# A gated-attention residual and LayerNorm kernel: the first group's own path through the statistics taken out, p added by VectorE or by accumulating transfers, and a new written order

## The chip, the cores and the metric

The kernel runs on one core of one Trainium2 chip. The metric is the device time of one execution in microseconds. One core has TensorE (PE; PEld are its weight loads), VectorE (DVE), ScalarE (ACT), GpSimd (POOL) and SyncE (SP), which here only issues transfers. Every engine works through its own instructions in the order in which they are written.

## The reference

The input x has 8 batches of 512 positions of 1024 values. Per batch, blocks of positions are summed, a key projection with Wk and a softmax over 8 blocks give weights, and the weighted block sum times Wo is one vector p per batch. All positions of the batch get it, then a LayerNorm and the residual follow:

```python
block_repr = inputs.reshape(B, n_blocks, block_size, H).sum(axis=2)
keys = jnp.einsum('bnh,kh->bnk', block_repr, Wk)
keys = keys / rms * rms_weight            # rms over the last axis
attn = jax.nn.softmax(jnp.einsum('bnh,h->bn', keys, q), axis=-1)
attended = jnp.einsum('bn,bnh->bh', attn, block_repr)
proj = jnp.einsum('bsh,kh->bsk', broadcast(attended), Wo)      # p
y = inputs + proj
out = (y - mu) / jnp.sqrt(var + EPS) * ln_gamma + ln_beta
return x + out
```

## The kernel before

The 8 batches form four groups of two. A group is 8 "rows" of work: a row is 128 partitions x 1024 values, and two rows make a tile of 1 MB. So there are 32 rows, 0 to 7 in the first group (group 0), 8 to 15 in group 1 and so on. They stay in the SBUF buffer xs, which has 26 places of one row (a weight tile takes one).

The loads come first: Wk, the four tiles of group 0, Wo, gamma, then the other groups as places come free. TensorE transposes the weights (L340, L351), sums blocks (L367, L389), projects (L411, L423) and spreads p over the partitions (L445, L499); the result is pb, one p per batch, in all partitions. Four rows of p go by four small GpSimd transfers into a table tab (L521).

Of a row of groups 1 to 3, `moments` adds p on VectorE and takes the row's sum in the same instruction (L556, called A here); ScalarE squares with that sum as bias (L559, the square). Several rows form a unit (UNITS: mostly four). For a unit GpSimd makes 1/std by a power, std by a product and writes columns into stat (`unit`, L627 to L635); TensorE transposes stat into lt. Then `results` ends a row: VectorE writes (gamma + std) * x into PSUM (L652, called B), TensorE adds the outer product of lt and tab (L642), ScalarE multiplies by 1/std into xs (L662), and SP stores two rows at once (L702). The last two rows go in halves (L674, L685).

Rows of group 0 go another way. Their own moments are taken by half-row statistics ahead of p, while the weights are still arriving (`x_moments`, L565, L567). p is not added to them; when p stands, one VectorE instruction per row takes the covariance with p (`x_cross`, L570, called C), p's moments come from L510 to L513, GpSimd joins them (`x_unit`, L582 to L597) and multiplies the table by a table of gamma (gtab, L525).

The order is not left to a scheduler. Each step is recorded with a number by `add`; the string ORDER lists the steps, each with a letter for its engine (G is GpSimd, S SP) and, behind an @, a place in xs or PSUM. A step is emitted, with all its instructions, where its token stands. Tokens like u4 are matrix products of zeros that nobody reads.

Of the kernel before, what the change touches and what calls it, by code (L numbers as in the profile page):

```python
# [9 lines left out]
AF = mybir.ActivationFunctionType  # L10
# [4 lines left out]
EPS = 1e-6  # L15
LAYER = 1
# [86 lines left out]
def block_attn_resid_kernel(  # L103
# [101 lines left out]
    cvt = alloc("cvt", [P, NX])
# [80 lines left out]
    for k in range(2):  # L286
        v = xpick[:, k, :].rearrange("p (r i m) -> p r i m", r=2, i=2)
        spots(v[:, :, :, 1 : 1 + GM], [[0, 2], [-2, 2], [0, GM]], -k, "xpick")
        for m in (0, GM + 1):
            spots(v[:, :, :, m : m + 1], [[0, 2], [0, 2], [0, 1]], -8, "xpick")  # L290
# [518 lines left out]
```

## Time and profile before

| | us |
|---|---|
| median of 3 runs (144.13 to 144.63) | 144.63 |
| the profiled execution | 144.32 |
| its span | 142.6 |
| PE busy (84%) | 119.7 |
| DVE busy (82%) | 116.6 |
| ACT busy (59%) | 83.9 |
| POOL busy (50%) | 71.3 |
| moved: 42.74 MB, mean over the span | 300 GB/s |

The profile shows one execution. Busy time is added over the whole span, so an engine at 82% may still be the limit of one stretch and idle in another. Between the profiled execution's own time and its span lie 1.7 us.

### The profile page before, as it was taken

What the parts mean: (1) busy time and instruction counts of PE and PEld (TensorE: products, weight loads), DVE (VectorE), ACT (ScalarE), POOL (GpSimd) and SP (SyncE); (2) the same over time, 40 slices, a digit from 0 to 9 for tenths busy, and PEclk for the clock granted to TensorE, in tenths of its full rate; (3) what the DMA queues carried; (4) which work ended last, traced back from release to release, by engine and by line L of the source; (5) the groups of instructions that cost most, each with busy time, mean ns of one, the idle gap of its engine ahead of it and who ended that gap; (6) DMA issues with size and microseconds to landing.
All of it is one profiled execution on the core that took longest, in us unless ns stands there. A gap on an engine that the chain in (4) does not pass through costs nothing.

```text
span 142.6 us, 2990 instructions
## 1 busy us (share of the span) xinstructions
PE 119.7 (84%) x1143; PEld 60.4 (42%) x1150; DVE 116.6 (82%) x194; ACT 83.9 (59%) x129; POOL 71.3 (50%) x106
## 2 busy tenths in 40 slices
PE   0999969999999996799999978998699774899920
PEld 0384439678865453334544242543243221323300
DVE  1269999999448997579999899999997999899900
ACT  3000050825833010173999979999978999699660
POOL 6881000000405788948223928993778069967100
PEclk9999999999999999879999999999959999999985
DMA  4999999999999998007785995617337708668894
GB/s 148 412 414 434 407 409 409 409 408 415 421 418 421 419 417 368 28 5 294 247 353 218 326 427 211 257 44 294 147 159 287 297 0 331 257 246 345 340 392 155
DMA packets 8286, 42.74 MB, mean 300 GB/s; under 512 B 1440, under 2 KB 1456, under 8 KB 4432
## 3 DMA queue, kind: packets, MB, share of 16 engines
q1 hardware_dynamic: 7632, 42.47, 73.8%
q8 instruction: 9, 0.15, 0.4%
q0 software_dynamic: 640, 0.08, 0.4%
q14 instruction: 5, 0.04, 0.1%
HBM read 25.71 MB, written 16.78 MB: 298 GB/s over the span
## 4 chain that ended last, share of the span: by engine, by line
DMA 29%; DVE 19%; PE 17%; POOL 16%; ACT 6%; issue 5%; SPq 2%; ACTq 0%; POOLq 0%; DVEq 0%
DMA xs<-in_L_cond_Wk_dram 11%; DMA xs<-in_x_dram 11%; DVE xs L556 11%; PE banks L642 7%; DMA xs<-in_L_cond_Wo_dram 7%; DVE banks L652 5%; PE banks L499 3%; ACT square L559 3%; PE banks L776 3%; POOL urs L631 3%; POOL stat L635 2%; POOL uv L629 2%; POOL ca L477 2%; PE banks L411 2%; DVE pb L570 2%
## 5 line engine op out<-in xcount | busy, mean ns | idle before, releaser
L652 DVE SCALAR_TENSOR_TENSOR banks<-gam,ustd,xs 128x1024 f32<-128x1024 f32 x30 | 38.7, 1320 | 1.9 <-ACT xs L662 0.9
L662 ACT ACTIVATE xs<-banks,urs 128x1024 f32<-128x1024 f32 x30 | 31.8, 1109 | 2.7 <-PE banks L642 2.3
L642 PE MATMUL banks<-tab,lt 32*128 32x512 f32 x128 | 27.8, 672 | 3.1 <-DVE banks L652 2.6
L556 DVE SCALAR_TENSOR_TENSOR xs<-xs,pb 128x1024 f32<-128x1024 f32 x24 | 28.8, 1220 | 0.9 <-ACT pb L167 0.8
L559 ACT ACTIVATE square<-xs,stat 128x1024 bf16<-128x1024 f32 x24 | 27.6, 1152 | 1.7 <-DVE xs L556 1.3
L776 PE MATMUL banks<-zeros 128*128 128x512 bf16 x69 | 20.3, 417 | 4.3 <-POOL blk L255 3.8
L477 POOL TENSOR_TENSOR ca<-cv,minus_half 128x8 f32<-128x8 f32 x4 | 9.5, 2382 | 27.8 <-DVE cv L475 27.7
L340 PE MATMUL banks<-ident,xs 128*128 128x128 f32 x120 | 15.7, 284 | 0.2 <-ACT wkT L167 0.2
L340 PEld LDWEIGHTS banks<-ident,xs 128*128 128x128 f32 x120 | 14.7, 195 | 2.7 <-issue 1.7
L411 PE MATMUL banks<-wkT,blkT 128*32 128x256 f32 x256 | 15.2, 381 | 0.4 <-DVE blkT L399 0.4
L167 ACT COPY wkT<-banks 128x1024 f32<-128x1024 f32 x3 | 2.9, 1015 | 21.0 <-PE banks L340 21.0
L642 PEld LDWEIGHTS banks<-tab,lt 32*128 32x128 f32 x128 | 8.3, 190 | 14.9 <-DVE banks L652 7.8
L521 POOL DMA_DIRECT2D tab<-pb x16 | 9.2, 577 | 9.6 <-ACT pb L167 9.6
L776 PEld LDWEIGHTS <-zeros 128*128 128x128 bf16 x74 | 6.9, 105 | 16.7 <-issue 8.9
L411 PE MATMUL banks<-woT,blkT 128*32 128x256 f32 x192 | 12.4, 397 | 0.0
L367 PE MATMUL banks<-xs,blk 128*32 128x256 f32 x192 | 12.2, 383 | 0.3 <-issue 0.3
L627 POOL COPY stat<-stat 128x4 f32<-128x4 f32 (+1 forms) x7 | 6.2, 879 | 10.2 <-DVE xs L556 5.1
L565 DVE BATCH_NORM_STATS2 bn<-xs 128x6 f32<-128x512 f32 x16 | 10.6, 686 | 0.2
L411 PEld LDWEIGHTS banks<-wkT,blkT 128*32 128x32 f32 x256 | 7.7, 110 | 6.3 <-DVE blkT L399 1.3
L570 DVE SCALAR_TENSOR_TENSOR pb<-xs,mv,pb 128x1024 f32<-128x1024 f32 x8 | 10.2, 1270 | 0.1
L629 POOL TENSOR_SCALAR uv<-ussq 128x4 f32<-128x4 f32 (+1 forms) x7 | 6.0, 864 | 5.6 <-ACT square L559 5.5
L631 POOL TENSOR_TENSOR urs<-uv,minus_half 128x4 f32<-128x4 f32 (+1 forms) x7 | 8.3, 1187 | 0.5
(103 smaller groups left out, 144.5 us busy)
## 6 DMA issues: line engine op xcount, KB each, us to landing
xs<-in_x_dram SPq DMA_DIRECT2D x16, 1024.0 KB, 13.1
out_dram<-xs SPq DMA_DIRECT2D x14, 1024.0 KB, 4.1
xs<-in_L_cond_Wk_dram SPq DMA_DIRECT2D x8, 512.0 KB, 13.1
xs<-in_L_cond_Wo_dram SPq DMA_DIRECT2D x8, 512.0 KB, 10.2
out_dram<-xs SPq DMA_DIRECT2D x2, 512.0 KB, 3.3
out_dram<-xs SPq DMA_DIRECT2D x4, 256.0 KB, 3.6
gam<-in_L_cond_ln_gamma_dram SPq DMA_DIRECT2D x1, 512.0 KB, 9.6
tab<-pb POOLq DMA_DIRECT2D x16, 4.0 KB, 3.5
```

The costliest lines, as they stand in the source:

```text
L340: nc.tensor.transpose(pair(name)[:, bass.ts(c, P)], xu(src)[:, c::HC], ident)
L367: nc.tensor.matmul(bank(name)[32 * j : 32 * j + 32, :QU], blk[G["g"]], xu(f"x{n}.{t}", r)[:, bass.ts(j, QU)], start=(t == 0 and r == 0), s ...
L411: nc.tensor.matmul(bank(name)[32 * j : 32 * j + 32, :QU], blkT[n % 2][:, c, :], wT[which][:, c, bass.ts(j, QU)], start=(c == 0), stop=(c = ...
L477: add("spow", "G", lambda _: nc.gpsimd.tensor_tensor(ca, cv, minus_half.to_broadcast([P, 8]), ALU.pow), reads=["cv", "minus_half"], writes ...
L556: add("A", "D", lambda _: nc.vector.scalar_tensor_tensor(x_row(k), x_row(k), 1.0, pb[n % 2], ALU.mult, ALU.add, accum_out=total), reads=pb ...
L559: add("Sq", "A", lambda _: nc.scalar.activation(square, x_row(k), AF.Square, bias=total, scale=-float(H), accum_out=ussq[u][:, r : r + 1]) ...
L570: add("C", "D", lambda _: nc.vector.scalar_tensor_tensor(pb[1], x_row(k), mv[:, k, 0:1], pb[0], ALU.subtract, ALU.mult, accum_out=cov[:, k ...
L631: add("upow", "G", lambda _: nc.gpsimd.tensor_tensor(rs, v, minus_half.to_broadcast([P, U]), ALU.pow), reads=[f"uv{u}", "minus_half"], wri ...
L642: nc.tensor.matmul(pair(name)[:, h * HALF : (h + 1) * HALF], lt_rows[lo : lo + 32, :], tab[n % NTAB][lo : lo + 32, :], start=False, stop=T ...
L652: add("B", "D", lambda _, j=j: nc.vector.scalar_tensor_tensor(pair(names[j]), gam, ustd[u][:, r + j : r + j + 1], x_row(k + j), ALU.add, A ...
L662: add("out", "A", lambda _, j=j: nc.scalar.activation(x_row(k + j), pair(names[j]), AF.Identity, scale=urs[u][:, r + j : r + j + 1]), read ...
L776: nc.tensor.matmul(banks[:, i, :], zeros[:, :P], zeros, start=True, stop=True)
```

## The change

1. The first group's own path is gone: no half-row statistics ahead of p, no covariance, no p moments, no gtab. All rows use `moments` and `unit`.
2. For the 8 rows in SENT (rows 4 to 7 and 12 to 15) p is not added by VectorE. GpSimd issues one accumulating transfer per tile (two rows), which adds pb to xs in place (`sent`). The sum of such a row is the sum of x (`row_sum`, on VectorE or ScalarE, possible before p) plus the sum of p (`p_sum`); `mean_columns` joins them into stat. The square is taken as before (`sent_squares`). The first group's units become 2, 2 and 4 rows, so that the sent rows are a unit.
3. std is a power (0.5) of its own instead of a product with 1/std, and stands ahead of 1/std. The statistics are kept in another scale (gamma is multiplied once by SC), so that the step uv is an addition alone.
4. The steps usum and uv can go to ScalarE, ust to VectorE, and three of the four last half outputs are done by VectorE.
5. ORDER is new throughout.

The core of the diff:

```diff
-UNITS = ((4,4),(4,4),(4,4),(4,2,2))
+SC = 2.0**15
+UNITS = ((2,2,4),(4,4),(4,4),(4,2,2))
+SENT = (4,5,6,7,12,13,14,15)
...
     def gamma_rows():
...
+        add("gsc", "AD", lambda e: nc.scalar.mul(gam, gam, SC) if e == "A" else nc.vector.tensor_scalar(gam, gam, SC, None, ALU.mult),
+            writes=["gam"])
...
-    def x_moments(k):
-        for i in range(2):
-            add("bn5", "D", lambda _, i=i: nc.vector.bn_stats(out=bn[:, i, :], in_=x_row(k)[:, i * HALF : (i + 1) * HALF]),
...
-    def x_cross(k):
-        add("C", "D", lambda _: nc.vector.scalar_tensor_tensor(
-            pb[1], x_row(k), mv[:, k, 0:1], pb[0], ALU.subtract, ALU.mult, accum_out=cov[:, k : k + 1]),
...
+    def row_sum(k):
+        add("Sx", "AD", lambda e: nc.scalar.activation(square, x_row(k), AF.Identity, accum_out=sx[:, k : k + 1]) if e == "A"
+            else nc.vector.tensor_reduce(sx[:, k : k + 1], x_row(k), AX.X, ALU.add),
+            reads=xk(k), writes=[f"sx{k}"])
+
+    def p_sum(G):
+        n = G["n"]
+        add("Sx", "AD", lambda e: nc.scalar.activation(square, pb[n % 2], AF.Identity, accum_out=sp[:, n : n + 1]) if e == "A"
...
+    def sent(k):
...
+        if row % 2 == 0:
+            def go(_):
+                at = plan.at[t]
+                nc.gpsimd.dma_start(out=xs[:, at : at + 2, :], in_=pb[n % 2].unsqueeze(1).to_broadcast([P, 2, H]),
+                                    accum_op=ALU.add)
+            add("dadd", "G", go, reads=pb_keys(n), writes=xk(k) + xk(k + 1))
+
+    def sent_squares(k):
+        q, r = unit_of[k]
+        u, i = q % NU, q % NST
+        add("Sq", "A", lambda _: nc.scalar.activation(
+            square, x_row(k), AF.Square, bias=stat[i][:, r, 0, 0:1], scale=-float(H), accum_out=ussq[u][:, r : r + 1]),
+            reads=xk(k) + [f"stat{i}.{r}"], writes=[f"ussq{u}.{r}"])
...
     def unit(q):
...
-        add("usum", "G", lambda _: nc.gpsimd.tensor_copy(st[:, :, 1, 0:1], st[:, :, 0, 0:1]),
-            reads=S4 + [f"stat{i}"], writes=[f"stat{i}.sum"])
-        add("uv", "G", lambda _: nc.gpsimd.tensor_scalar(v, ssq, 1.0 / H**3, EPS, ALU.mult, ALU.add),
-            reads=Q4, writes=[f"uv{u}"])
-        add("upow", "G", lambda _: nc.gpsimd.tensor_tensor(rs, v, minus_half.to_broadcast([P, U]), ALU.pow),
-            reads=[f"uv{u}", "minus_half"], writes=[f"urs{u}"])
-        add("ustd", "G", lambda _: nc.gpsimd.tensor_tensor(std, v, rs, ALU.mult),
-            reads=[f"uv{u}", f"urs{u}"], writes=[f"ustd{u}"])
+        if first not in SENT:
+            add("usum", "GA", lambda e: (nc.gpsimd.tensor_copy if e == "G" else nc.scalar.copy)(st[:, :, 1, 0:1], st[:, :, 0, 0:1]),
+                reads=S4 + [f"stat{i}"], writes=[f"stat{i}.sum"])
+        add("uv", "GA", lambda e: nc.gpsimd.tensor_scalar(v, ssq, EPS * H**3, None, ALU.add) if e == "G"
+            else nc.scalar.activation(v, ssq, AF.Identity, bias=epsc),
+            reads=Q4 + ["epsc"], writes=[f"uv{u}"])
+        add("upow", "G", lambda _: nc.gpsimd.tensor_tensor(
+            std, v, halves[:, 0:1].to_broadcast([P, U]), ALU.pow),
+            reads=[f"uv{u}", "halves"], writes=[f"ustd{u}"])
...
+        add("upow", "G", lambda _: nc.gpsimd.tensor_tensor(
+            rs, v, halves[:, 1:2].to_broadcast([P, U]), ALU.pow),
+            reads=[f"uv{u}", "halves"], writes=[f"urs{u}"])
```

ORDER decides what stands behind what on each engine. Three places, before and after (line numbers differ between the two kernels):

ScalarE from the end of p of group 0 on. pb_90 is p of group 0 and 2, pb_91 of group 1 and 3; kj is the key square of group 1's softmax, ce its exponential. Before:

```order
L167 COPY pb_90<-banks 128x384
L167 COPY pb_90<-banks 128x128
L464 ACTIVATE kj,sd<-banks 128x256
L167 COPY lt_83<-banks 128x256
L482 ACTIVATE ce,es<-cs,mx 128x8
L662 ACTIVATE xs<-banks,urs_119 128x1024 x2
L167 COPY pb_91<-banks 128x512 x2
L559 ACTIVATE square,ussq_113<-xs,stat_81 128x1024
L662 ACTIVATE xs<-banks,urs_119 128x1024 x2
```

And now:

```order
L545 ACTIVATE square,sx<-xs 128x1024
L551 ACTIVATE square,sp<-pb_90 128x1024
L540 ACTIVATE square,ussq_107<-xs,stat_81 128x1024 x2
L615 COPY stat_81<-stat_81 128x2
L618 ACTIVATE uv_111<-ussq_107,epsc 128x2
L545 ACTIVATE square,sx<-xs 128x1024
L540 ACTIVATE square,ussq_108<-xs,stat_82 128x1024 x2
L582 ACTIVATE stat_81<-sx,sp 128x8
L168 COPY lt_83<-banks 128x128
L451 ACTIVATE kj,sd<-banks 128x256
L570 ACTIVATE square,ussq_109<-xs,stat_81 128x1024
L654 ACTIVATE xs<-banks,urs_115 128x1024 x2
```

Seven full-row passes (L545 and L551 are sums, L540 the squares of rows 0 to 3) and small steps of the units stand between p and the key square. Behind it comes the square of row 4, a sent row (L570), ahead of the first two outputs (L654). Before, the key square, lt and the exponential were all that stood ahead of the first outputs (L662).

GpSimd from p of group 0 on. ca is the power of a softmax. Before:

```order
L521 DMA tab_92<-pb_90 2x512 x3
L582 TENSOR_SCALAR stat_81<-mv,mvp 128x8
L521 DMA tab_92<-pb_90 2x512
L582 TENSOR_SCALAR stat_82<-mv,mvp 128x8
L589 TENSOR_SCALAR cvt<-cov,mvp 128x4
L591 TENSOR_TENSOR uv_115<-cvt,mv 128x4
L593 TENSOR_TENSOR urs_119<-uv_115,minus_half 128x4
L595 TENSOR_TENSOR ustd_123<-uv_115,urs_119 128x4
L525 TENSOR_TENSOR tab_92<-tab_92,gtab 128x512
L597 COPY stat_81<-ustd_123 128x8
L477 TENSOR_TENSOR ca<-cv,minus_half 128x8
```

And now:

```order
L501 DMA tab_92<-pb_90 2x512 x2
L563 DMA xs<-pb_90 128x2x1024
L501 DMA tab_92<-pb_90 2x512
L563 DMA xs<-pb_90 128x2x1024
L501 DMA tab_92<-pb_90 2x512
L620 TENSOR_TENSOR ustd_119<-uv_111,halves 128x2
L627 TENSOR_TENSOR urs_115<-uv_111,halves 128x2
L615 COPY stat_82<-stat_82 128x2
L617 TENSOR_SCALAR uv_112<-ussq_108 128x2
L620 TENSOR_TENSOR ustd_120<-uv_112,halves 128x2
L627 TENSOR_TENSOR urs_116<-uv_112,halves 128x2
L464 TENSOR_TENSOR ca<-cv,halves 128x8
```

The two accumulating transfers (L563: first rows 6 and 7, then 4 and 5) stand among the four table transfers; the last two of the table are issued behind one and both of them. The first unit (119, 115) has only its two powers left here.

VectorE from p of group 0 to the first row B of a sent unit. Before, the eight C (L570) stood here with the moments of p (L510 to L513) among them. Now:

```order
L537 SCALAR_TENSOR_TENSOR xs,stat_81<-xs,pb_90 128x1024 x2
L546 TENSOR_REDUCE sx<-xs 128x1
L386 STREAM_TRANSPOSE blkT_86<-banks 128x256
L537 SCALAR_TENSOR_TENSOR xs,stat_82<-xs,pb_90 128x1024 x2
L623 TENSOR_TENSOR stat_81<-ustd_119,ind_75 128x4x3
L644 SCALAR_TENSOR_TENSOR banks<-gam,ustd_119,xs 128x1024 x2
L453 SCALAR_TENSOR_TENSOR vj,sd<-banks,qw 128x256
L456 TENSOR_TENSOR sdd<-diag_69,sd 128x16
L546 TENSOR_REDUCE sx<-xs 128x1
L623 TENSOR_TENSOR stat_82<-ustd_120,ind_75 128x4x3
L462 TENSOR_SCALAR cv<-banks 128x8
L644 SCALAR_TENSOR_TENSOR banks<-gam,ustd_120,xs 128x1024 x2
```

L537 is A for rows 0 to 3, L546 the sums of two sent rows of group 1, L623 the columns of stat, L644 is B for rows 0 to 3. The rest of the second softmax (group 1) comes behind these rows.

## Rows read from the trace of the kernel before

**Rows 1.** The page: busy tenths, DMA share and GB/s in 40 slices of the span

```profile
DVE  1269999999448997579999899999997999899900
ACT  3000050825833010173999979999978999699660
...
DMA  4999999999999998007785995617337708668894
GB/s 148 412 414 434 407 409 409 409 408 415 421 418 421 419 417 368 28 5 294 247 353 218 326 427 211 257 44 294 147 159 287 297 0 331 257 246 345 340 392 155
```

**Rows 2.** Windows: busy us (x instructions) of each engine, clock, DMA share, GB/s

```profile
43.90:66.20 22.30, 19.86 (x279) 9.59 (x274) 18.81 (x35) 4.45 (x10) 17.75 (x18) 0.92 0.66 273
66.20:135.20 69.00, 60.41 (x514) 24.44 (x519) 66.41 (x102) 62.31 (x96) 42.80 (x49) 0.98 0.63 251
135.20:142.60 7.40, 1.18 (x4) 0.29 (x2) 0.00 (x0) 2.48 (x4) 0.00 (x0) 0.68 0.73 281
```

**Rows 3.** Timeline of ACT: start us, us, operation, count, idle before it

```profile
42.63 1.29 ACT L167 COPY pb<-banks 128x512 f32<-128x512 f32 x3 [0.83 <-PE banks L445]
...
75.68 1.15 ACT L559 ACTIVATE square<-xs,stat 128x1024 bf16<-128x1024 f32 x1
...
76.95 1.15 ACT L559 ACTIVATE square<-xs,stat 128x1024 bf16<-128x1024 f32 x1
...
86.52 1.15 ACT L559 ACTIVATE square<-xs,stat 128x1024 bf16<-128x1024 f32 x1
...
87.67 2.10 ACT L662 ACTIVATE xs<-banks,urs 128x1024 f32<-128x1024 f32 x2
89.66 1.14 ACT L559 ACTIVATE square<-xs,stat 128x1024 bf16<-128x1024 f32 x1
...
135.12 2.56 ACT L685 ACTIVATE xs<-banks,urs 128x512 f32<-128x512 f32 x4 [0.37 <-PE banks L642]
```

**Rows 4.** The chain of waits in order of time: start us, us, what

```profile
30.84 15.37 DMA xs<-in_x_dram
...
66.24 1.23 DVE xs L556 x2
```

**Rows 5.** Timeline of SP's queue: the first store

```profile
63.89 0.35 SPq L702 DMA_DIRECT2D out_dram<-xs  x1
```

**Rows 6.** Groups by line: busy us, mean ns of one, idle before

```profile
L565 DVE BATCH_NORM_STATS2 bn<-xs 128x6 f32<-128x512 f32 x16 | 10.6, 686 | 0.2
L570 DVE SCALAR_TENSOR_TENSOR pb<-xs,mv,pb 128x1024 f32<-128x1024 f32 x8 | 10.2, 1270 | 0.1
L477 POOL TENSOR_TENSOR ca<-cv,minus_half 128x8 f32<-128x8 f32 x4 | 9.5, 2382 | 27.8 <-DVE cv L475 27.7
...
L570 DVE DVE_READ_ACCUMULATOR pb<-xs,mv,pb 128x1 f32 x8 | 0.7, 82 | 0.0
...
L510 DVE BATCH_NORM_STATS2 bnp<-pb 128x6 f32<-128x512 f32 x2 | 1.4, 694 | 1.2 <-ACT pb L167 1.2
...
L482 ACT ACTIVATE ce<-cs,mx 128x8 f32<-128x8 f32 x4 | 1.2, 298 | 2.2 <-DVE mx L481 2.2
```

**Rows 7.** Timeline of POOL: the first table issues and one unit's steps

```profile
44.21 1.79 POOL L521 DMA_DIRECT2D tab<-pb  x3 [6.19 <-ACT pb L167]
...
93.85 1.05 POOL L629 TENSOR_SCALAR uv<-ussq 128x4 f32<-128x4 f32 x1
94.98 1.04 POOL L631 TENSOR_TENSOR urs<-uv,minus_half 128x4 f32<-128x4 f32 x1
96.10 0.30 POOL L633 TENSOR_TENSOR ustd<-uv,urs 128x4 f32<-128x4 f32 x1
96.47 1.15 POOL L635 TENSOR_TENSOR stat<-ustd,ind 128x24 f32<-128x24 f32 x1
```

**Rows 8.** The page's DMA issues: count, size of one, median us to landing

```profile
out_dram<-xs SPq DMA_DIRECT2D x14, 1024.0 KB, 4.1
...
tab<-pb POOLq DMA_DIRECT2D x16, 4.0 KB, 3.5
```

More of the change, by code (lines that the diff above doesn't have):

```diff
@@ L282, in block_attn_resid_kernel @@
         v = gpick[:, k, :].rearrange("p (r i m) -> p r i m", r=2, i=2)
-        spots(v[:, :, :, 0:1], [[0, 2], [-2, 2], [-1, 1]], -k, "gpick", -1.0 / H)
+        spots(v[:, :, :, 0:1], [[0, 2], [-2, 2], [-1, 1]], -k, "gpick", -SC / H)
         spots(v[:, :, :, GM + 1 : GM + 2], [[0, 2], [-2, 2], [-1, 1]], -4 - k, "gpick")
-    fill(xpick, 0.0, "xpick")
[L286 to L290, printed above, removed]
     for g in sizes:
@@ L296, in block_attn_resid_kernel @@
         fill(ind[g][:, GM : GM + 1], 1.0, f"ind{g}")
-    fill(minus_half, -0.5, "minus_half")
+    fill(epsc, EPS * H**3, "epsc")
+    fill(halves[:, 0:1], 0.5, "halves")
+    fill(halves[:, 1:2], -0.5, "halves")
     for i in range(NST):
@@ L321, in vectors @@
                 frees=["gbr"] if i == NTAB - 1 else [])
-        def grows(_):
-            for k in range(2):
-                nc.tensor.matmul(bank("gxr")[:, k * QU : (k + 1) * QU], xpick[:, k, :], gb, start=True, stop=True)
-        add("gbr", "P", grows, reads=["xpick", "gb", "gb1"], claim=("ps", "gxr", 1))
-        add("c512", "AD", lambda e: copy(e, gtab, bank("gxr")), writes=["gtab"], use=["gxr"], frees=["gxr"])
     def gamma_rows():
@@ L351, in go @@
                     nc.tensor.transpose(bank(name)[:, bass.ts(c, P)], xu(src)[:, 4 * i + c :: HC], ident)
-            add("Th", "P", go, reads=[f"{src}.0", "ident"], claim=("ps", name, 1), frees=[src] if i else [])
+            add("Th", "P", go, reads=[f"{src}.0", "ident"], writes=[f"{src}.half"], claim=("ps", name, 1), frees=[src] if i else [])
             add("c512", "AD", lambda e_, i=i, name=name: copy(
@@ L557, in moments @@
             x_row(k), x_row(k), 1.0, pb[n % 2], ALU.mult, ALU.add, accum_out=total),
-            reads=pb_keys(n), writes=xk(k) + [f"stat{i}.{r}"])
+            reads=pb_keys(n) + [f"stat{i}"], writes=xk(k) + [f"stat{i}.{r}"])
         add("Sq", "A", lambda _: nc.scalar.activation(
@@ L561, in moments @@
             reads=xk(k) + [f"stat{i}.{r}"], writes=[f"ussq{u}.{r}"])
-    def x_moments(k):
-        for i in range(2):
-            add("bn5", "D", lambda _, i=i: nc.vector.bn_stats(out=bn[:, i, :], in_=x_row(k)[:, i * HALF : (i + 1) * HALF]),
-                reads=xk(k), writes=[f"bn{i}"])
-        add("bna", "D", lambda _: nc.vector.bn_aggr(out=mv[:, k, :], in_=bn), reads=["bn0", "bn1"], writes=[f"mv{k}"])
-    def x_cross(k):
-        add("C", "D", lambda _: nc.vector.scalar_tensor_tensor(
-            pb[1], x_row(k), mv[:, k, 0:1], pb[0], ALU.subtract, ALU.mult, accum_out=cov[:, k : k + 1]),
-            reads=pb_keys(0) + [f"mv{k}"] + xk(k), writes=[f"cov{k}", "v0.pa", "v0.pc", "v0.pd"])
@@ new lines, in row_sum @@
+    def row_sum(k):
[5 more added lines that the diff above has]
+        add("Sx", "AD", lambda e: nc.scalar.activation(square, pb[n % 2], AF.Identity, accum_out=sp[:, n : n + 1]) if e == "A"
+            else nc.vector.tensor_reduce(sp[:, n : n + 1], pb[n % 2], AX.X, ALU.add),
+            reads=pb_keys(n), writes=[f"sp{n}"])
@@ new lines, in mean_columns, with go @@
+    def mean_columns(q):
+        first, U = units[q]
+        i = q % NST
+        n = place[first][0]["n"]
+        def go(e):
+            o, a, b = stat[i][:, :U, :, 0], sx[:, first : first + U].unsqueeze(2).to_broadcast([P, U, 2]), sp[:, n : n + 1]
+            if e == "A":
+                nc.scalar.activation(o, a, AF.Identity, bias=b)
+            else:
+                nc.gpsimd.tensor_scalar(o, a, b, None, ALU.add)
+        add("umean", "GA", go,
+            reads=[f"sx{k}" for k in range(first, first + U)] + [f"sp{n}", f"stat{i}"],
+            writes=[f"stat{i}.{r}" for r in range(U)] + [f"stat{i}.sum"])
@@ L650, in results @@
         names = [f"row{k + j}" for j in range(2)]
+        t, keys = table_of(k)
         for j in range(2):
@@ L658, in go @@
                 for h in range(2):
-                    outer(names[j], lts[i][:, r // 2, :], 32 * (2 * ((r + j) % 2) + h), n, h)
-        add("O2", "P", go, reads=[f"lt{i}"] + tab_keys(n), use=names)
+                    outer(names[j], lts[i][:, r // 2, :], 32 * (2 * ((r + j) % 2) + h), t, h)
+        add("O2", "P", go, reads=[f"lt{i}"] + keys, use=names)
         for j in range(2):
@@ L672, in result_in_halves @@
         cols = [slice(h * HALF, (h + 1) * HALF) for h in range(2)]
+        t, keys = table_of(k)
         for h in range(2):
@@ L679, in result_in_halves @@
             lo = 32 * (2 * (r % 2) + h)
-            add("Oh", "P", lambda _, h=h, lo=lo: outer(name, lts[i][:, r // 2, :], lo, n, h),
-                reads=[f"lt{i}"] + tab_keys(n), writes=[f"{name}.{h}"])
+            add("Oh", "P", lambda _, h=h, lo=lo: outer(name, lts[i][:, r // 2, :], lo, t, h),
+                reads=[f"lt{i}"] + keys, writes=[f"{name}.{h}"])
         for h in range(2):
@@ L709, in set_bits, with send @@
         add("bits", "P", go, reads=["zeros"] + w_keys(1, range(8)), claim=("ps", f"bits{t}", 2))
+    def send(G):
+        ks = [k for k in SENT if place[k][0] is G]
+        if ks:
+            p_sum(G)
+        for k in ks:
+            sent(k)
     for what in LOADS.split():
@@ L721, in block_attn_resid_kernel @@
     to_columns(G0)
-    for k in range(NX):
-        x_moments(k)
+    for k in SENT:
+        if place[k][0] is G0:
+            row_sum(k)
     for e in range(8):
@@ L763, in block_attn_resid_kernel @@
             load_x(G, t)
+    for k in SENT:
+        if place[k][0]["n"]:
+            row_sum(k)
     for q, (first, U) in enumerate(units):
@@ L767, in block_attn_resid_kernel @@
             attention(G)
+        if first in SENT:
+            mean_columns(q)
         for k in range(first, first + U):
-            (moments if G["n"] else x_cross)(k)
-        (unit if G["n"] else x_unit)(q)
+            if k in SENT:
+                sent_squares(k)
+            else:
+                moments(k)
+        unit(q)
         if q:
```

75 lines of the change are left out of this document (21 added, 54 removed), and 55 rows, old and new, of the table ORDER.

## Prediction

> **What bounds the kernel now.** I read the page first. Its slices of 3.57 us show two halves [rows 1]: up to 57 us the transfers move 400 to 430 GB/s without a break (weights and x), then two slices at 28 and 5 GB/s, then stores. VectorE (DVE) is at 9 tenths or more nearly throughout the second half, ScalarE (ACT) does almost nothing between slices 12 and 17. The windows say the same in numbers [rows 2]: from the moment p of the first two batches stands (43.9 us, the end of the three ACT copies that start at 42.63 [rows 3]) to 66.2 us, ACT works 4.5 of 22.3 us; from 66.2 to 135.2 us DVE is busy 66.4 of 69.0, ACT 62.3, and DVE sets the pace. The chain of waits confirms the first half: transfers to 46.2 us, and at 66.24 it turns to VectorE's additions [rows 4]. The first store is issued only at 63.89 [rows 5]: before it come the instructions C of VectorE, a row of GpSimd steps and the multiplied table.
>
> So after 43.9 us the end is set by the engine with the most work, plus its idle time, plus what follows it. Today that is VectorE: 43.9 + 85.2 busy + 6.1 idle (3.5 before 66.2, 2.6 after) + 7.4 from its last instruction to the end = 142.6. The prediction fills in the same four terms. The profiled execution took 144.32 us, span 142.6, so 1.7 us lie around the span; the median of three is 144.63.
>
> **The change, part by part.**
>
> *Off VectorE.* The 16 half-row statistics and their aggregates (10.6 us busy [rows 6] for the former) run before p, beside the loads; there their loss is worth nothing, as the transfers end p's chain. After p the 8 instructions C go. With their accumulator reads they are busy 10.2 + 0.7 = 10.9 us. The moments of p go too, two half-row statistics (1.4 [rows 6]) and two small ones: 1.7. New after p are two row sums (price: C is the nearest row of 1024 elements, 1.2 each: 2.4), four small multiplications into stat (0.2 each, 0.8) and three half outputs (0.65 each from 2.56 for four [rows 3], 2.0). The additions A stay 24 in number: rows 0 to 3 gain them, 12 to 15 lose them. VectorE after p: 85.2 - 12.6 + 5.2 = 78 us. The scaling of gam, one full-row pass of about 1.2 us, stands ahead of p between cv and cs, where VectorE waits for GpSimd's power (mean 2.4 us [rows 6]): nothing; without that cover 1.2 us.
>
> *Onto ScalarE.* Starts in [rows 3] give the pitches: a square followed by a square 1.27 us (75.68 to 76.95), followed by something else 1.15 (86.52 to 87.67), an output 1.0 (two in 87.67 to 89.66). Eight more squares (rows 0 to 7), about 1.2 each: 9.7. Two row sums and two sums of p after p (full-row passes with an accumulator, so priced as squares): 5.1. Twelve small steps taken from GpSimd: nearest row is the exponential with 0.30 us busy [rows 6], bounds 0.1 and 0.3, I take 0.2: 2.4. Three half outputs go to VectorE: -1.9. ScalarE was 4.5 + 62.3 + 2.5 = 69.3 after p [rows 2] and becomes 84.6 by this; adding up its list pitch by pitch gives 83.6, which I take. **It becomes the engine with the most work, 83.6 against 78**; now it is VectorE with 85.2.
>
> *Off GpSimd.* One unit of four now costs 1.05 + 1.04 + 0.30 + 1.15 us from last square to finished stat [rows 7]. The sum step and scaling go to ScalarE, the product that made std is replaced by a power of its own (about 1.0), and 1/std moves behind it. That shortens a unit by about 1 us. Units are written ahead of their use, so this only covers waits; I count it in the idle time.
>
> *The time of p* I leave at 43.9 us. Its last weights arrive as now; TensorE takes some parts of the product earlier, ScalarE scales two of the three parts instead of one. Either moves it by 1 us at most (the copies of p take 1.29 in all [rows 3]), and ScalarE's first new pass waits for a tile of group 1 that lands 2.5 us (1 MB) before 46.21 [rows 4] in any case.
>
> *An earlier start.* ScalarE no longer waits for the group's statistics. Its new order from 43.9 us is: row sum, sum of p, two squares, two small steps, row sum, two squares, one small step, copy of lt, square of keys: five passes at 1.27, two at 1.15, 0.7 for the small ones, 0.25 and 0.36: 9.96 us. At **53.9 us** it stands at the first square of a sent row (row 4).
>
> *The accumulating transfers.* The trace has none. GpSimd issues table, table, transfer, table, transfer, table; an issue is 0.6 us (three in 1.79 [rows 7]), so the first transfer is issued from 45.4 and moves from 46.0. For the bytes the nearest row is an ordinary transfer of the same 1 MB: at 410 GB/s [rows 1] 2.56 us of all engines; a store takes 4.1 us from issue to landing [rows 8], so about 1 us is landing. Lower bound: both are served at once, 46.0 + 5.1 + 1 = 52.1, no wait. Upper bound: they read the row and p and write the row, 3 MB each instead of 1, 7.7 us, and share the engines with the loads that run until 57 us: everything is through at 57 + 15.4 = 72. I take the plain price, as its row is the nearest, and equal turns with the loads: 46.0 + 2 x 5.1 + 1 = **57.2 us**. ScalarE asks at 53.9 for row 4, whose transfer is issued second, and so waits 3.3 us; everything behind is queued: both first outputs, three squares, the exponential of the second softmax. TensorE waits there too: the last quarter of the first table is issued behind both transfers on the same queue, and the first four outer products need it.
>
> *The second pair* is issued at about 68 us; ScalarE needs it some 9 us after p of group 1. By the same prices it lands 6 to 11 us after its issue: a wait of 0 to 3.7 us, I take 1.
>
> **The sum.** Now the bound engine idles 2.6 of 69.0 us [rows 2], 3.8%; over 83.6 us that is 3.2. From the end of ScalarE's list to the end of the span there are now 142.6 - 137.7 = 4.9 us (135.12 + 2.56 [rows 3]); VectorE's half outputs add 0.5. So 43.9 + 83.6 + 3.2 + 3.3 + 1.0 + 5.4 = 140.4 us of span, **142.1 us** of time: 2.2 us or 1.5% less than this execution.
>
> **Rivals.**
>
> *A: the accumulating transfers come late; slower.* Place: ScalarE's square of row 4. Price: what one transfer occupies. The span breaks even with 5.5 us of waits in both places, the first transfers landing at about 59.4, so 3.1 us for each at equal turns: only a fifth above the plain price. If each counts as two streams read (5.1 us), the first pair lands at 46.0 + 20.4 + 1 = 67.4, ScalarE stands still from 53.9 for 13.5 us and the second wait is 3.7: 153.3 us of span, 155 us. At 3.85 us the waits are 8.5 and 2: 148.3. For it: the loads fill 9 tenths or more of every slice up to 57 us [rows 1], and more bytes are read than written. Against: after 57 us they are all but idle, so the second transfer has them alone, and an accumulation may not be dearer than a copy. The Trainium skill (Collectives: The Full Stack, "The bandwidth ceiling: the fold count and why AG ≠ RS ≠ AR") says that an addition in the transfer needs two source reads on the same ring and so gets about half the rate; by that rule the time would be the 155 us of this rival. No run here shows it.
>
> *B: no wait at all.* The transfers are served ahead of the loads (52.1). Then 43.9 + 83.6 + 3.2 + 5.4 = 136.1, 137.8 us. For it: the 4 KB tables, issued between 44 and 48 us into a full queue of loads, are no exception to a median landing of 3.5 us [rows 8]. Against: 1 MB is 256 times as much.
>
> *C: no change.* ScalarE and VectorE, now 83.6 and 78 us, wait for each other more than today: ScalarE idles not 3.2 but 5.4 us beside the forecast waits, or the transfers cost their break-even price. Then the time stays within 0.5% of 144.3 (0.7 us, about what a measurement can tell).
>
> **How the numbers follow.** Forecast (waits of 1 to 5 us) 0.34, B 0.18, C 0.10, A 0.38. Faster by more than 0.5% is forecast and B, 0.52; same C, 0.10; slower A, 0.38. The range runs from B with a little less idle time (137.0) into A as far as a price of about 4.6 us (152.0); what is left out is the dear end of A, some 0.12, and 0.06 below. The likeliest case alone has 140 to 143.5. I put the forecast on the faster side because three of the four terms fall, by rows: the bound engine's work by 1.6 us, its idle time without the transfers by 2.9, what follows it by 2.0; against these 6.5 stand only the waits for the transfers.
>
> **What would show it.** Right: ScalarE without long gaps from 43.9 us on; a gap of 2 to 5 us before the square of row 4, released by a transfer; the first store at about 60; 84 us of ScalarE work after p; no VectorE instruction C, its busy time near 99 us instead of 116.6. Wrong: the gap exceeds 6 us (A) or is missing (B); transfers of a measured length above 3 us each; the granted clock falling in that gap; or ScalarE busy under 90% after 66 us without a transfer as releaser (C). It would be wrong altogether if VectorE still set the pace.

## The result, and the profile after

The changed kernel takes **179.07 us** (median of four runs, 176.43 to 181.01), the kernel before 144.63: a ratio of 1.228, interval (95%) 1.215 to 1.241. Two of the four runs, and some of those further on, fell into a slower state that a part of the executions show; ratios and intervals leave such runs out, so that a ratio isn't always the quotient of the medians. The profiled execution took 176.43 us, its span is 174.7. The forecast was 142.1, its range ended at 152.0. Of the rivals, A has the right place and the right mechanism, but its 155 us are 21 us short of this execution.

The page of the changed kernel, same columns as [rows 1], here in slices of 4.37 us; PEclk is the granted clock in tenths:

```profile
DVE  2349972431985000177960007667997779899670
ACT  2033530487991002968970059619899957999740
PEclk9999999999999555599999755559996557957995
DMA  5999999999999993268799995053347280096595
GB/s 209 398 427 419 409 407 411 415 417 424 418 356 299 331 261 66 105 221 328 178 191 298 243 371 240 4 241 123 124 173 308 120 360 4 2 383 251 240 379 195
```

Two holes: in slices 14 and 15, and again in 22 and 23, neither VectorE nor ScalarE works. Over both the DMA row is at 9, yet the line below it stands at 243 to 331 GB/s instead of over 400: the engines are as full as before and move a fifth to two fifths less. The granted clock falls to 5 tenths in the first hole and at the end of the second, and stays there for some slices behind each.

The timeline of ScalarE (start, length, operation, count, idle before it and its releaser), to be laid beside [rows 3]:

```profile
42.54 1.12 ACT L168 COPY pb<-banks 128x512 f32<-128x512 f32 x2 [0.88 <-PE banks L432]
...
52.78 0.38 ACT L451 ACTIVATE kj<-banks 128x256 bf16<-128x256 f32 x1
...
68.95 1.15 ACT L570 ACTIVATE square<-xs,stat 128x1024 bf16<-128x1024 f32 x1 [15.70 <-DMA xs<-pb]
...
81.15 1.07 ACT L168 COPY pb<-banks 128x512 f32<-128x512 f32 x2 [0.74 <-PE banks L486]
...
102.31 1.15 ACT L570 ACTIVATE square<-xs,stat 128x1024 bf16<-128x1024 f32 x1 [11.44 <-DMA xs<-pb]
```

p of the first group stands at 43.6 us (ScalarE's next step starts at 43.63) and the list runs to 53.2 without a hole; then it stops before the first square of a sent row, 15.7 us in the first group and 11.4 in the second. p of the second group comes only at 82.

GpSimd's issues, and the first store of SyncE's queue (answering [rows 5, 7]):

```profile
45.50 1.33 POOL L563 DMA_DIRECT2D xs<-pb  x1
46.31 1.12 POOL L501 DMA_DIRECT2D tab<-pb  x1
46.88 1.80 POOL L563 DMA_DIRECT2D xs<-pb  x1
47.67 1.61 POOL L501 DMA_DIRECT2D tab<-pb  x1
...
83.18 2.57 POOL L563 DMA_DIRECT2D xs<-pb  x2
```

```profile
72.42 0.35 SPq L695 DMA_DIRECT2D out_dram<-xs  x1
```

The first store moved from 63.89 to 72.42 us. The list of waits (engine, line, releaser: us in total, times, longest), and two pieces of the chain of waits (start, us):

```profile
ACT square L570 <- DMA xs<-pb: 27.1, 2, 15.7
DVE cv L462 <- PE banks L460: 22.0, 4, 18.6
DVE banks L644 <- ACT xs L654: 15.6, 4, 12.3
PE banks L633 <- DMA tab<-pb: 15.1, 1, 15.1
```

```profile
47.67 21.36 DMA tab<-pb
...
83.99 18.21 DMA xs<-pb
```

Where [rows 4] turned from transfers to VectorE, the chain now runs over two transfers, 39.6 us of it. The 15.1 us of TensorE is a table of 4 KB: its last piece is issued at 47.67, behind both accumulating transfers on one queue, and lands when they do. VectorE's waits are the echo: it waits for TensorE and ScalarE, which wait for the transfers.

Windows with the columns of [rows 2] (the fourth ends with ScalarE's list, the last is what follows):

```profile
56.00:68.00 12.00, 0.00 (x0) 0.00 (x0) 0.00 (x0) 0.00 (x0) 0.00 (x0) 0.55 0.95 257
102.30:110.00 7.70, 4.93 (x26) 1.35 (x26) 3.60 (x8) 7.69 (x14) 0.00 (x0) 0.50 0.59 247
110.00:116.00 6.00, 6.00 (x29) 2.96 (x28) 4.11 (x4) 2.29 (x4) 2.57 (x3) 0.50 0.26 104
43.60:167.70 124.10, 89.84 (x786) 37.18 (x778) 77.28 (x125) 83.30 (x142) 52.97 (x57) 0.77 0.66 225
167.70:174.70 7.00, 1.19 (x4) 0.29 (x2) 1.99 (x4) 0.14 (x1) 0.00 (x0) 0.66 0.70 268
```

In the same four terms as the prediction: 43.6 to p + 83.3 of ScalarE's work + 40.8 idle + 7.0 behind its list = 174.7. Of the idle time 27.1 us are the two holes, 13.7 us lie elsewhere. The groups [rows 6] no longer hold C; in its place stand

```profile
L537 DVE SCALAR_TENSOR_TENSOR xs<-xs,pb 128x1024 f32<-128x1024 f32 x24 | 28.5, 1217 | 2.2 <-ACT pb L168 2.1
L570 ACT ACTIVATE square<-xs,stat 128x1024 bf16<-128x1024 f32 x8 | 9.2, 1146 | 27.2 <-DMA xs<-pb 27.1
```

and VectorE's busy time is 101.0 us (forecast: near 99). On the page, the queue of software-driven transfers (packets, MB, share of 16 engines' span) and the landing of the transfers, beside [rows 8]:

```profile
q0 software_dynamic: 1728, 4.28, 13.2%
...
xs<-pb POOLq DMA_DIRECT2D x4, 1024.0 KB, 16.9
```

13.2% of 174.7 us is 23.1 us of all 16 engines. The tables alone have 0.4% of it (the run without the transfers, below), so that each of the four transfers takes 12.8% / 4, or **5.6 us**; it had been priced at 2.56.

### The profile page after: what moved, and what is told of

Its sections match the earlier page's. It is cut to its first block, busy times and chain, and to the rows that moved or that the text cites. A ratio compares the mean times of both kernels' runs of the same rounds, so it can differ in the third digit from the quotient of the medians.

```text
span 174.7 us, 2944 instructions
## 1 busy us (share of the span) xinstructions
PE 129.7 (74%) x1131; PEld 63.3 (36%) x1131; DVE 101.0 (58%) x163; ACT 100.7 (58%) x166; POOL 61.0 (35%) x86
## 3 DMA queue, kind: packets, MB, share of 16 engines
q0 software_dynamic: 1728, 4.28, 13.2%
## 4 chain that ended last, share of the span: by engine, by line
DMA 36%; PE 28%; POOL 10%; issue 9%; ACT 9%; DVE 4%; SPq 1%; POOLq 0%; ACTq 0%; DVEq 0%
DMA tab<-pb 12%; DMA xs<-pb 10%; PE banks L633 7%; DMA xs<-in_L_cond_Wo_dram 7%; DMA xs<-in_x_dram 7%; PE banks L398 6%; PE banks L327 4%; ACT xs L654 4%; ACT square L540 4%; PE banks L486 4%; POOL ca L464 3%; POOL ustd L620 2%; PE banks L410 2%; PE banks L354 2%; POOL urs L627 2%
## 5 line engine op out<-in xcount | busy, mean ns | idle before, releaser
L644 DVE SCALAR_TENSOR_TENSOR banks<-gam,ustd,xs 128x1024 f32<-128x1024 f32 x30 | 37.6, 1290 | 17.9 <-ACT xs L654 15.6
L633 PE MATMUL banks<-tab,lt 32*128 32x512 f32 x128 | 31.2, 830 | 21.4 <-DMA tab<-pb 15.1
L654 ACT ACTIVATE xs<-banks,urs 128x1024 f32<-128x1024 f32 x30 | 32.0, 1105 | 5.2 <-PE banks L633 2.7
L537 DVE SCALAR_TENSOR_TENSOR xs<-xs,pb 128x1024 f32<-128x1024 f32 x24 | 28.5, 1217 | 2.2 <-ACT pb L168 2.1
L540 ACT ACTIVATE square<-xs,stat 128x1024 bf16<-128x1024 f32 x24 | 27.6, 1150 | 0.6
L464 POOL TENSOR_TENSOR ca<-cv,halves 128x8 f32<-128x8 f32 x4 | 8.8, 2198 | 50.7 <-DVE cv L462 50.7
L570 ACT ACTIVATE square<-xs,stat 128x1024 bf16<-128x1024 f32 x8 | 9.2, 1146 | 27.2 <-DMA xs<-pb 27.1
L786 PE MATMUL banks<-zeros 128*128 128x512 bf16 x59 | 18.7, 459 | 5.4 <-POOL blk L250 4.3
L620 POOL TENSOR_TENSOR ustd<-uv,halves 128x4 f32<-128x4 f32 (+1 forms) x10 | 11.8, 1183 | 30.0 <-ACT uv L618 29.6
L354 PE MATMUL banks<-xs,blk 128*32 128x256 f32 x192 | 14.8, 446 | 7.9 <-DMA xs<-in_x_dram 7.9
L501 POOL DMA_DIRECT2D tab<-pb x16 | 10.9, 692 | 17.1 <-DVE pb L170 7.5
L327 PEld LDWEIGHTS banks<-ident,xs 128*128 128x128 f32 x120 | 15.1, 195 | 3.9 <-issue 1.7
L627 POOL TENSOR_TENSOR urs<-uv,halves 128x4 f32<-128x4 f32 (+1 forms) x10 | 13.6, 1360 | 0.0
L168 ACT COPY wkT<-banks 128x1024 f32<-128x1024 f32 x5 | 5.1, 1014 | 12.6 <-PE banks L327 12.6
L354 PEld LDWEIGHTS banks<-xs,blk 128*32 128x32 f32 x192 | 5.8, 121 | 16.4 <-DMA xs<-in_x_dram 8.8
## 6 DMA issues: line engine op xcount, KB each, us to landing
xs<-in_L_cond_Wo_dram SPq DMA_DIRECT2D x8, 512.0 KB, 10.5
gam<-in_L_cond_ln_gamma_dram SPq DMA_DIRECT2D x1, 512.0 KB, 10.5
```

The lines of the kernel that those rows point to most:

```text
L327: nc.tensor.transpose(pair(name)[:, bass.ts(c, P)], xu(src)[:, c::HC], ident)
L354: nc.tensor.matmul(bank(name)[32 * j : 32 * j + 32, :QU], blk[G["g"]], xu(f"x{n}.{t}", r)[:, bass.ts(j, QU)], start=(t == 0 and r == 0), s ...
L464: add("spow", "G", lambda _: nc.gpsimd.tensor_tensor(ca, cv, halves[:, 1:2].to_broadcast([P, 8]), ALU.pow), reads=["cv", "halves"], writes ...
L537: add("A", "D", lambda _: nc.vector.scalar_tensor_tensor(x_row(k), x_row(k), 1.0, pb[n % 2], ALU.mult, ALU.add, accum_out=total), reads=pb ...
L540: add("Sq", "A", lambda _: nc.scalar.activation(square, x_row(k), AF.Square, bias=total, scale=-float(H), accum_out=ussq[u][:, r : r + 1]) ...
L620: add("upow", "G", lambda _: nc.gpsimd.tensor_tensor(std, v, halves[:, 0:1].to_broadcast([P, U]), ALU.pow), reads=[f"uv{u}", "halves"], wr ...
```

## The experiments

All times are medians; the kernel before took 144.3 to 144.8 us beside them.

**Without the transfers.** In `sent` (L563) the transfer is left out; rows 4 to 7 and 12 to 15 are computed without p, all else is the changed kernel.

```
-                nc.gpsimd.dma_start(out=xs[:, at : at + 2, :], in_=pb[n % 2].unsqueeze(1).to_broadcast([P, 2, H]),
-                                    accum_op=ALU.add)
+                pass
```

> The changed kernel with the four accumulating transfers left out, so that rows 4 to 7 and 12 to 15 are computed without p; everything else, the order included, is untouched. Theory T (the transfers land late, each 4 KB packet taking twice the time of a copied one and taking turns with the loads): both gaps of ScalarE ahead of the squares of rows 4 and 12 (15.7 and 11.4 us) go, and with them what followed, and the time is that of the forecast without waits, 136 to 142 us. Rival O (the new order is itself slow, with the 11.5 us that the two gaps do not account for): the gaps go, but the time stays at 148 us or more.

Measured: **143.04 us**, ratio 0.988 (0.982 to 0.995). Windows of its span of 141.5 us:

```profile
44.10:104.00 59.90, 54.74 (x697) 25.88 (x689) 51.44 (x88) 57.51 (x103) 34.28 (x36) 1.00 0.72 282
104.00:134.70 30.70, 24.95 (x92) 8.87 (x90) 25.64 (x37) 25.26 (x40) 14.99 (x18) 0.72 0.53 216
134.70:141.50 6.80, 1.06 (x3) 0.23 (x2) 1.86 (x3) 0.02 (x1) 0.00 (x0) 0.75 0.70 269
```

The two holes are gone; the time is 1 us above T's range and 5 us below O's. So the four transfers cost 34.6 us by the ratios (36.0 by the medians), and everything else in the change together gains 1.2%, with eight additions of p left out. From p to 104 us ScalarE is idle 2.4 of 59.9 us, as the forecast had it (4%); in the next 30.7 us it is idle 5.4.

**Plain transfers.** The same transfer without the addition: p is copied over the rows, so the sum is missing from eight rows.

```
-                nc.gpsimd.dma_start(out=xs[:, at : at + 2, :], in_=pb[n % 2].unsqueeze(1).to_broadcast([P, 2, H]),
-                                    accum_op=ALU.add)
+                nc.gpsimd.dma_start(out=xs[:, at : at + 2, :], in_=pb[n % 2].unsqueeze(1).to_broadcast([P, 2, H]))
```

> The four transfers stay, on the same queue, but copy p over the rows instead of adding it (these rows then hold p alone). It separates the price of a packet from the turns with the loads. Theory T: the packets fall from 0.327 to about 0.16 us, 32 packets on each engine taking turns with loads of 0.313 still need 32 x 0.47 = 15 us instead of 20.5, so the first gap falls by about 5 us to 10 or 11, the second to about 6; 163 to 169 us. Rival P (only the second read matters, the queue of the loads does not): the first gap falls below 4 us, the second goes; below 152 us. Rival F (a fixed delay of this queue): no change, 174 us or more.

Measured: 159.31 us (one run). Its queue and its waits:

```profile
q0 software_dynamic: 1728, 4.28, 7.0%
```

```profile
ACT square L569 <- DMA xs<-pb: 10.2, 1, 10.2
PE banks L632 <- DMA tab<-pb: 9.6, 1, 9.6
```

Less the tables' 0.4% that is 6.6% of 157.6 us over four transfers, 2.6 us each, the 2.56 of the forecast. As many packets and bytes with the addition take 5.6: **twice the time**. The first hole of 10.2 us hit the expectation. The second was expected at 6 us and is missing, so the run came out faster than 163. But even at the plain price the first wait would have been 10 us and not 3.3: the start and the turns beside the loads were mis-sized too.

**Loads held back.** Five loads of x (the third batch group and a tile of the fourth) wait on SyncE's queue until the first pair has landed, by two tiny copies from the accumulated rows into their place.

```
-... 150S@14 ... 151S@24 ... 152S@10 ... 153S@12 154S@16 ...
+... 137G 150S@14 151S@24 152S@10 153S@12 154S@16 ...
+            if name == "x2.0":
+                for j in (2, 3):
+                    nc.sync.dma_start(out=xs[0:1, i + j - 2, 0:8], in_=xs[0:1, plan.at[f"x0.{j}"], 0:8])
```

> The five 1 MB loads of x for the third batch group and the first tile of the fourth wait until the first pair of accumulating transfers has landed (two small copies from the accumulated rows into their place stand ahead of them on SyncE's queue). Theory T (packets take equal turns with those of the loads, 0.327 us beside 0.313 us): without the loads two transfers need 10.4 us of all engines from about 48 us, landing 57 to 61, and the gap before the square of row 4 is 4 to 8 us instead of 15.7; what the loads lose comes back behind it, as TensorE waits for x of the third group: 160 to 174 us in all. Rival L (the 20 us from issue to landing belong to the transfer itself: its start, its writes, its order): the gap stays at 13 us or more, and the time is 179 or above.

Measured: 178.9 us (one run). The hole before row 4 is 7.15 us, within T's 4 to 8 and far from the 13 of rival L; the time is above T's 160 to 174. The DMA view of 44 to 72 us, in 40 slices of 0.7 us:

```profile
DMA  4100499999999999999971000000769999999999
GB/s 176 59 12 0 82 181 187 181 187 170 199 193 167 196 187 193 217 176 187 193 123 18 6 0 12 0 0 0 129 222 445 421 410 421 445 433 398 456 433 410
```

This is the price by itself: with nothing beside them the two transfers fill the engines from 47 to 58.5 us and move some 190 GB/s; the loads behind them move over 400. They also start within 2 us of their issue (45.46). And it shows why holding the loads back doesn't help: they are issued at 62.9, and TensorE then waits 12.8 us for x of the third group (`PE banks L357 <- DMA xs<-in_x_dram` in its waits); the second hole is 16.3 us.

**Tables ahead.** The table pieces are issued ahead of both accumulating transfers (137G, 138G moved behind 141G; the same for the second group).

> All four table transfers of groups 0 and 1 are issued ahead of the two accumulating ones of the group; nothing else moves. TensorE then no longer waits for the last quarters of the tables behind the accumulating transfers. Theory T: ScalarE still meets the square of row 4 first, the transfers land within 1 us of where they did, and the outputs stay behind that square: 173 to 180 us, no gain beyond 3 us. Rival Q (the tables' place in the queue is what holds the kernel): the outputs and the second softmax go on, 160 us or less.

Measured: 182.4 us (one run), no gain, and 2 us above T's range. TensorE's wait for a table is no longer in the list, and `ACT square L570 <- DMA xs<-pb` is 31.8 us. So the tables' place in the queue gave a second wait beside the first and wasn't the cause.

**One pair at a time.** `if n == 0:`, or `if n == 1:`, ahead of the transfer in `sent`; the rows of the other pair are computed without p.

> Only the first pair of accumulating transfers (rows 4 to 7) is left; the second pair's p is left out (rows 12 to 15 go through the rest without p). Theory T (each transfer costs its own two-read price and its turns with the loads, so each pair has its own wait): the gap before the square of row 4 stays at 15 to 16 us, the gap of 11.4 us before the square of row 12 goes, and with it some of the low clock behind it: 161 to 166 us. Rival R (the second gap is mostly a consequence of the first: late loads, low clock): 172 us or more. Rival S (the second pair is the dearer one): 158 us or less.

> The counterpart of the run with the first pair alone: only the second pair of accumulating transfers (rows 12 to 15) is left, rows 4 to 7 go through the rest without p. Theory T (each pair has a wait of its own, and the two add up): no gap before the square of row 4, p of group 1 at about 64 us, the pair issued at about 66 and ScalarE asking at 73; two transfers of 5.4 us beside two or three loads land at 79 to 84, so the gap before the square of row 12 is 6 to 11 us and the time 152 to 160 us. Rival R (without the first gap the loads are through before and the pair is hidden, as my forecast's 1 us has it): gap under 3 us, 147 us or less.

Measured: first pair alone 161.84 us, second alone 159.08 (one run each). Their waits:

```profile
ACT square L571 <- DMA xs<-pb: 15.1, 1, 15.1
PE banks L634 <- DMA tab<-pb: 14.5, 1, 14.5
```

```profile
ACT square L571 <- DMA xs<-pb: 14.0, 1, 14.0
PE banks L354 <- DMA xs<-in_x_dram: 8.0, 1, 8.0
```

Against the run without transfers these are 18.8 and 16.0 us, together 34.8, and the four cost 34.6 by the ratios. As far as single runs can tell, the two pairs add up and neither is a consequence of the other. The second, issued at 65.3 us, is needed at 73.3 and lands at 87.3; I had expected a hole of 6 to 11 us, it is 14.0. TensorE also waits 8.0 us for x of a later group; these loads run on the same engines as the transfers.

**TensorE kept busy in the holes.** Products of zeros ahead of the waiting steps: 72 before 186P, 36 before 382P.

```
+    "... u7 u7 (72 times) 186P ... z6 z6 (36 times) 382P ..."
```

> As the changed kernel, with 72 products of zeros (128x512) for TensorE in the first gap and 36 in the second, so that it isn't idle while it waits. Theory T (of the 38 us some 11 are not gaps but their consequence, of which the granted clock of 0.50 behind each gap is a part): granted clock 1.00 behind both gaps, 2 to 7 us less than the changed kernel: 172 to 177 us. Rival N (TensorE isn't what the stretches behind the gaps wait for): within 1% of the changed kernel, 177 to 181 us.

Measured: **172.47 us**, ratio 1.172 (1.162 to 1.183) against 1.228 (1.215 to 1.241): 8 us less by the ratios, a little more than T's 2 to 7 and against rival N. The profiled execution took 175.65 us, hardly less than that of the changed kernel, so its lines show the clock and not where the 8 us were gained. TensorE's timeline behind the first hole, here and in the changed kernel:

```profile
70.29 1.14 PE L633 MATMUL banks<-tab,lt 32*128 32x512 f32 x8
71.36 1.07 PE L354 MATMUL banks<-xs,blk 128*32 128x256 f32 x16
```

```profile
69.17 2.08 PE L633 MATMUL banks<-tab,lt 32*128 32x512 f32 x4 [15.07 <-DMA tab<-pb]
71.17 1.94 PE L354 MATMUL banks<-xs,blk 128*32 128x256 f32 x16
```

The holes are about as long as before (15.0 us the first, 10.4 the second), but the same 16 products behind the first take 1.07 us instead of 1.94. T's clock of 1.00 came behind the first hole alone: behind the second it is 0.76 in 104 to 110 us, where it was 0.50, and 0.50 again in 110 to 116, so that one was mended in part.

**The addition on VectorE instead.** Three versions without transfers that compute all rows in full. First, one VectorE addition per row right before its square (the sums of rows and of p stay on their engines):

```
+            nc.vector.tensor_tensor(x_row(k), x_row(k), pb[n % 2], ALU.add)
             nc.scalar.activation(square, x_row(k), AF.Square, ...)
```

> The same as the changed kernel, but the 8 rows get p by one VectorE addition each, written right ahead of the row's square; no accumulating transfer. VectorE's work after p becomes 78 + 8 x 1.2 = 87.6 us and sets the pace again. Theory T: 43.9 + 87.6 + 3 to 6 idle + 6 = 141 to 144 us of span, 142 to 146 us of time, about that of the kernel before. Rival O: 150 us or more.

Measured: 149.75 us, ratio 1.032 (1.025 to 1.038): between the ranges of T and O. Second, the sum in the same pass, early in VectorE's list, without row sums and sums of p:

```
+                for j in (k, k + 1):
+                    nc.vector.scalar_tensor_tensor(x_row(j), x_row(j), 1.0, pb[n % 2], ALU.mult, ALU.add,
+                                                   accum_out=sx[:, j : j + 1])
```

> No accumulating transfers; p is added to the eight rows by VectorE with the row's sum in the same instruction (as for all other rows), early in VectorE's list instead of right before the square; the eight row sums and two sums of p fall away. Theory T (the work of the engines sets the time once no transfer is waited for: ScalarE about 77 us after p, VectorE about 86): 142 to 146 us, as the kernel before within 1.5%. Rival W (in-order waits between VectorE and ScalarE cost as much as in the run with the additions right before the squares): 148 us or more.

Measured: 151.15 us, ratio 1.047 (1.039 to 1.056): rival W's side. TensorE's timeline shows one place where time is lost:

```profile
76.14 1.13 PE L628 MATMUL banks<-tab,lt 32*128 32x512 f32 x4 [1.08 <-DVE banks L639]
78.98 0.61 PE L460 MATMUL banks<-sdd,same 128*128 128x16 f32 x2 [1.71 <-DVE sdd L456]
79.52 3.64 PE L398 MATMUL banks<-woT,blkT 128*32 128x256 f32 x32
```

The sums of the next softmax wait for VectorE, which is at the additions; they start at 78.98 instead of 74.21 in the run without transfers, and right behind them 32 products take 3.64 us instead of 1.93. Third, the additions of rows 6, 7 and 12 to 15 moved behind those few instructions (217D 218D 138D; 306D 237D; 309D 238D):

> As the run with p added in VectorE's one pass (no transfers), but the additions of rows 6, 7 and 12 to 15 stand behind the few instructions of VectorE on which the next softmax rests. Theory T (there the additions delayed the next p by 2 us in group 1 and by 5 us in group 2, where TensorE then fell to a granted clock of 0.60): 144 to 147 us. Rival W (the eight additions cost their 9.8 us wherever they stand, as VectorE is full): 149 us or more.

Measured: 147.1 to 153.2 us in four runs, too scattered for a verdict. No version with the addition on VectorE beats the kernel before.

**The 5 us that have nothing to do with transfers.** 20 products of zeros in the run without transfers, ahead of 376P (nine), 405P (six) and 426P (five); rows 4 to 7 and 12 to 15 again without p.

> As the run with the transfers left out (rows 4 to 7 and 12 to 15 without p; there 143.0 us, 0.988 of the kernel before, where a forecast without any wait gave 137.8 us), with 20 more products of zeros (128x512) for TensorE in three places where it waits for VectorE or GpSimd near 100, 105 and 118 us and the granted clock is 0.50 right behind. Theory T (part of the 5 us by which the forecast without waits is too low is the low clock behind these waits): clock 1.00 there, 1 to 3 us less, 0.968 to 0.981 of the kernel before. Rival N (these stretches wait for VectorE and ScalarE, not for TensorE): 0.984 to 0.993, no difference.

Measured: 146.0 us, ratio 1.014 (1.008 to 1.020): slower than without them, which neither theory had. Its TensorE timeline:

```profile
106.67 2.19 PE L785 MATMUL banks<-zeros 128*128 128x512 bf16 x6 [1.58 <-DVE vw L442]
108.79 2.04 PE L486 MATMUL banks<-vw,spread 64*128 64x256 f32 x8
```

The six products ahead of 405P didn't run in the wait but after it, at 0.37 us each, and p of the last group came 2 us later. As the filling delayed the work, the run doesn't tell whether the low clock matters there.

## Why the prediction was wrong, step by step

*Right.* p at 43.9 us: 43.6. ScalarE becomes the engine with the most work, 83.6 us behind p: 83.3. VectorE 78: 77.3 + 2.0 behind ScalarE's list, 79.3. First transfer issued from 45.4: 45.50. ScalarE stands at row 4 at 53.9: 53.2. C and the moments are gone, and GpSimd's shortened units are no one's bound. The place of the loss is the one that rival A names.

*Wrong: "I take the plain price, as its row is the nearest", 2.56 us.* An accumulating transfer occupies the engines for 5.6 us where the same transfer as a copy takes 2.6, a factor of 2.1; the price of a copy was right. The run with the loads held back shows it directly, some 190 GB/s beside more than 400 for loads. The Trainium skill (Collectives: The Full Stack, "The bandwidth ceiling: the fold count and why AG ≠ RS ≠ AR") gives two source reads and about half the rate for the addition in a collective; the factor of 2.1 agrees with that, while the reads themselves show in no run here. The nearest row was the wrong guide here: a store and a load show one read and one write, and the text itself noted that more is read than written.

*Wrong: "moves from 46.0 ... equal turns with the loads ... 57.2".* With loads in front the pair landed at 68.9. Two things were missing. The transfers began late. On the changed kernel's DMA view of 44 to 72 us, in slices of 0.7 us,

```profile
DMA  9999999999999999999999999999999943100000
GB/s 433 421 386 410 433 427 369 445 363 322 281 345 275 310 287 328 339 293 304 269 304 357 389 299 360 310 258 228 246 240 234 193 82 59 18 0 0 12 0 0
```

the rate falls from over 400 to about 300 GB/s only near 50 us, while with the loads held back the transfers start within 2 us. The kernel before had shown this delay: the first group's four tables, issued beside the loads from 44.21 us on, took 5.2 us to land (median in its DMA view of 43 to 48 us). They are the longest of its 16 tables:

```profile
DMA to landing us min/median/max: 1.6/3.5/5.3
```

So rival B's "no exception to a median landing of 3.5 us" was misread, and the start at 46.0 was too early. And as each transfer needed twice as long, it also took turns with the loads for twice as long. Rival A's own sum, 67.4, was off by only 1.5 us, in part by luck: its transfers start some 4 us too early, but it gives them 21.4 us to the landing, where from 50 to 68.9 us it was 18.9. Plain copies still made ScalarE wait 10.2 us: the 3.3 us of the forecast were out of reach even at the plain price.

*Wrong: "The second pair ... lands 6 to 11 us after its issue: a wait of 0 to 3.7 us, I take 1".* Measured 19 us from issue (83.2 to 102.3) and 11.4 of waiting. I had taken the engines for free by then [rows 1]; but later x loads and stores run at just that time, and with the first hole gone it was no better: 22 us, a wait of 14.0.

*Wrong: the idle time, "over 83.6 us that is 3.2".* Measured 13.7 us beside the two holes. Without transfers it is 7.8 (2.4 before 104 us, 5.4 after), so 4.6 us of this miss belong to the rule of proportion. That part is the most of why the no-wait case takes 143 us and not rival B's 137.8. Rival C had VectorE and ScalarE wait for each other; that isn't shown. In the 5.4 us of that run ScalarE waits directly for TensorE (2.9 us, at a granted clock of 0.72) or for nothing that the profile names (2.4), as in

```profile
108.86 1.07 ACT L168 COPY pb<-banks 128x512 f32<-128x512 f32 x2 [2.04 <-PE banks L486]
...
132.02 2.12 ACT L653 ACTIVATE xs<-banks,urs 128x1024 f32<-128x1024 f32 x2 [1.28 <-issue]
```

The remaining 5.9 us come with the holes. The list of waits of the changed kernel has

```profile
ACT pb L168 <- PE banks L486: 6.6, 4, 2.3
ACT xs L654 <- PE banks L633: 2.7, 3, 1.4
```

9.3 us of waiting for TensorE behind p, against 4.1 without the transfers. The low clock behind the holes can account for that, as TensorE kept busy gives back 8 us. That late loads have a share was only argued from TensorE's waits for them. The last term, 5.4 us behind ScalarE's list, is 7.0 (6.8 without transfers).

*Rival A's 155 us* against a span of 153.3 lack 2.2 us in the first wait, 7.7 in the second, 10.5 of idle time and 1.6 at the end, 22.0, less 0.3 + 0.3 for p and the work: 21.4, which is 174.7. Its chance of 0.38 was too low, and cutting the range at a price of 4.6 us left out its own price of 5.1, which is near what was measured. Its break-even (3.1 us each; the 5.5 us of waits beside it are the first wait alone, with 1.0 in the second place it is 6.5) was the number to look at: a forecast that holds only up to a price a fifth above the cheapest bound is not the likeliest.

What stays open: the idle time without transfers was located (5.4 of 7.8 us in the last 30 us) but not removed, where TensorE kept busy gains its 8 us was not traced, and whether the transfers could be hidden by moving the sent rows' squares behind the next p was not tried.

## What to carry to other kernels

Price an accumulating transfer as two transfers, add its turns with whatever the DMA engines carry in the same stretch, take its start from the landings in just that stretch and not from a median over the kernel, and look up who needs the result and what is queued behind that instruction: here 8 VectorE passes of 1.2 us were exchanged for 22 us of all DMA engines, in front of an in-order list. Compute the price at which the gain is gone, and if it lies close to the cheapest estimate, forecast the other side. A long wait of TensorE costs more than its length: look at the granted clock behind it, and fill the wait, but only where the filling ends before the wait does.

## What the runs showed of the hardware

- Adding while transferring halves the rate: 5.6 against 2.6 us of all engines for 1 MB, some 190 GB/s alone against over 400 for loads.
- Beside a stretch full of loads the software queue starts late: the tables issued in 44 to 45.3 us land after 5.6 us in the changed kernel and after 1.8 us with the loads held back (medians of two).
- A full DMA row says nothing of bytes: in 56 to 68 us the engines are busy 0.95 of the time at 257 GB/s.
- Small transfers behind large ones on the same software queue land with them: the 4 KB table issued at 47.67 us took 21.4 us, where [rows 8] has a median of 3.5.
- Standing still in 56 to 68 us, TensorE fell to a granted clock of 0.50, the lower of its two levels (1.2 GHz); behind the second hole it worked at 0.50 from 102.3 to 116 us. 108 products of zeros gave back 8 us by the ratios. Six in the wrong place, in the run without transfers, held up p of the last group by 2 us.
